# A two-layer masked attention kernel: TensorE's order fixed with projections between attention stages, units of eight heads, transposed value product

## The chip, the cores and the metric

One NeuronCore of one Trainium2 chip runs the kernel. The metric is the device time of one execution in microseconds; the kernel before takes 4095.5 us (median of 4 runs, 4094.55 to 4097.6).

TensorE does the matrix products and the transposes, VectorE, ScalarE and GpSimd the rest. The traces list each engine's instructions in an order of its own and put a wait down to the engine that ended it: the transposes of the probabilities, for one, waited 124.5 us in the kernel before, 122.3 of them for ScalarE. In both kernels TensorE writes its results to buffers in PSUM; the copy out of one is called an eviction below, and the program uses the buffer again only after it.

## The reference, cut to what matters

128 batches of 128 tokens with 512 features pass two layers, all in f32:

```python
# layer 0: 4 heads of 64
q, k, v = split_heads(x @ Wq), split_heads(x @ Wk), split_heads(x @ Wv)
sim  = where(adj, q k^T / 8, -max);  out = softmax(sim) v
x = layernorm(x + out @ Wo + bo)
# layer 1: 8 heads of 64, with a norm in front and the diagonal always allowed
h = layernorm(x) * gamma + beta
q, k, v = split(h @ w_qkv.T)
scores = where(adj | eye, q k^T / 8, -1e9);  out = softmax(scores) v
x = layernorm(x + out @ w_out.T + b_out)
```

## The kernel before

Four batches (512 tokens) form a group, and there are 32 groups. The tokens of a group are transposed to xT, projected to qk and v, and then every batch goes through stages: scores and softmax, transposes of the probabilities, value product, transposes of its result, output product with the norm. Layer 0 of one group runs in turns with layer 1 of the group before it. A scheduler, which works with its own guess of times, puts every engine's instructions in order.

```python
def scores(l, g, b):
    ...
    for h in range(H):
        nc.tensor.matmul(ps[:, h % 2, h // 2, :], qk[r, h // 2, t], qk[r, H // 2 + h // 2, t], ...)
    nc.gpsimd.memset(sm, (NEG0, NEG1)[l])
    for s in range(2):
        nc.vector.copy_predicated(sm[:, s], mask..., ps[:, s, :H // 2, :])
    nc.vector.tensor_reduce(nmax, sm, AX.X, ALU.max, negate=True)
    ... # one Exp per head on ScalarE, with its sum
def attend(l, g, b):
    for h in range(H):
        nc.tensor.matmul(pm[:, h * D:(h + 1) * D], pT[:, h, :], v[:, b, h * D:(h + 1) * D], ...)
    nc.vector.tensor_mul(a..., pm..., rec...)
def attended_t(l, g, b):
    ... # TensorE transposes of a, ScalarE copies them to aT
def residual(l, g, b):
    nc.gpsimd.tensor_tensor(xb, xin, (bias0, bias1)[l], op=ALU.add)
    ... # output product: aT, WO
    nc.vector.tensor_add(y, pm, xb)
    norm_stats(y, 0, mv)
    r = rstd_of(mv, 1)                      # two small GpSimd instructions
    nc.vector.tensor_scalar(y, y, mv[:, 0, 0:1], r, op0=ALU.subtract, op1=ALU.mult)
STAGES = (scores, probs_t, attend, attended_t, residual)
```

## Time and profile before

| engine | busy us | share | instructions |
|---|---|---|---|
| TensorE, matmuls | 3890.9 | 95% | 16193 |
| VectorE | 1654.0 | 40% | 3366 |
| ScalarE | 1139.0 | 28% | 4013 |
| GpSimd | 755.3 | 18% | 1095 |

TensorE's busy time here says how long something was in it, not how fast it went: 3891 us busy, where its instructions at their undisturbed distances make 3523 (the sum is told below). So two further things are read below: what the idle time before an instruction was waiting for, and the clock that TensorE was granted (mean 0.967 before). In the traces of both kernels the clock is either full or half (1.0 or 0.5 in all 132 records before and 258 after), so the time at half clock is about 2 x (1 - mean) x span: 2 x 0.033 x 4095 = 270 us before.

Here are two groups of the view of groups. The columns are: line, engine, operation, tiles, shape and count; busy us and mean ns of one; idle time of the engine before them, and what ended it.

```profile
L252 PE MATMUL o<-wo,aT 128*128 128x512 f32 x1536 | 768.3, 630 | 2.6 <-ACT aT L226 1.8 <-DVE x L255 0.8
...
L259 DVE TENSOR_SCALAR x<-x,mv,rstd 128x512 f32<-128x512 f32 x128 | 68.8, 537 | 48.1 <-POOL rstd L239 48.1
```

The output product (o) hardly ever waits, and VectorE's normalizing instruction takes 537 ns.

### The profile page before, as it was taken

The numbers are of one execution on the slowest core, as the hardware profiler recorded it, in microseconds if no ns is written. First come the engines' busy times: TensorE is split into PE (matmuls) and PEld (weight loads), VectorE is DVE, ScalarE is ACT, GpSimd is POOL, SyncE is SP. The second block draws the span as 40 slices with busy tenths as digits, with TensorE's granted clock in tenths as the row PEclk, the third lists the DMA queues.
The fourth block names the chain that finished last, engine by engine and source line by source line (L and its number), as shares of the span: only waits on it lengthen the run. The fifth ranks groups of instructions, "written<-read, shape, count | busy, mean of one in ns | idle before, by whom it ended". The sixth has DMA issues, their size and how long they took to land.

```text
span 4094.8 us, 42881 instructions
## 1 busy us (share of the span) xinstructions
PE 3890.9 (95%) x16193; PEld 2270.6 (55%) x16193; DVE 1654.0 (40%) x3366; ACT 1139.0 (28%) x4013; POOL 755.3 (18%) x1095
## 2 busy tenths in 40 slices
PE   8999999999999999999999999999999999999998
PEld 5555555555555555555555555555555555555554
DVE  3343443434434334334344343443434434334443
ACT  2322322223323133232232222322313323223222
POOL 1121211212212112112121121221211211112120
PEclk8999999999999999999999999999999999999998
DMA  3000000000000000000000000000000000000000
GB/s 100 12 22 11 22 17 17 22 11 22 22 14 19 16 17 22 17 17 22 11 22 17 16 22 11 22 19 14 22 11 22 22 14 19 21 12 22 6 13 14
DMA packets 56894, 78.78 MB, mean 19 GB/s; under 512 B 19816, under 2 KB 21360, under 8 KB 56688
## 3 DMA queue, kind: packets, MB, share of 16 engines
q1 hardware_dynamic: 56688, 76.04, 5.4%
q8 instruction: 128, 2.10, 0.2%
q14 instruction: 78, 0.64, 0.1%
HBM read 42.47 MB, written 33.55 MB: 19 GB/s over the span
## 4 chain that ended last, share of the span: by engine, by line
PE 72%; DVE 13%; POOL 7%; ACT 4%; issue 3%; DMA 1%; POOLq 0%; ACTq 0%
PE qk L134 33%; PE v L148 16%; PE o L252 8%; PE av L211 4%; PE xt L118 3%; PE sc L170 3%; DVE sm L175 3%; ACT sm L182 3%; PE pt L196 3%; POOL rstd L239 3%; POOL xb L249 2%; DVE nmax L178 2%; POOL sm L173 2%; DVE h L271 1%; DVE y L255 1%
## 5 line engine op out<-in xcount | busy, mean ns | idle before, releaser
L134 PE MATMUL qk<-xT,w 128*128 128x512 f32 x3072 | 1364.2, 601 | 0.0
L134 PEld LDWEIGHTS qk<-xT,w 128*128 128x128 f32 x3072 | 582.1, 193 | 674.9 <-issue 665.1
L249 POOL TENSOR_TENSOR xb<-x,bias 128x512 f32<-128x512 f32 x256 | 324.4, 1267 | 2776.4 <-DVE x L255 1577.2
L252 PE MATMUL o<-wo,aT 128*128 128x512 f32 x1536 | 768.3, 630 | 2.6 <-ACT aT L226 1.8
L182 ACT ACTIVATE sm<-sm,nmax 128x128 f32<-128x128 f32 x1536 | 595.0, 390 | 462.5 <-DVE nmax L178 461.4
L148 PE MATMUL v<-w,xT 128*128 128x256 f32 (+1 forms) x2048 | 670.9, 486 | 0.0
L148 PEld LDWEIGHTS v<-w,xT 128*128 128x128 f32 x2048 | 389.1, 190 | 285.0 <-issue 260.2
L141 DVE COPY qk<-qk 128x512 f32<-128x512 f32 x96 | 66.4, 692 | 959.5 <-PE qk L134 959.5
L196 PE MATMUL pt<-ident,sm 128*128 128x128 f32 x1536 | 317.9, 306 | 124.5 <-ACT sm L182 122.3
L150 DVE COPY v<-v 128x512 f32<-128x512 f32 x192 | 132.8, 692 | 747.4 <-PE v L148 747.4
L226 ACT COPY aT<-at 128x256 f32<-128x256 f32 (+1 forms) x256 | 121.8, 476 | 1117.1 <-PE at L224 1116.6
L252 PEld LDWEIGHTS o<-wo,aT 128*128 128x128 f32 x1536 | 288.3, 203 | 253.4 <-issue 230.8
L211 PE MATMUL av<-v,pT 128*128 128x64 f32 x3072 | 378.2, 274 | 0.2 <-DVE pT L202 0.2
L211 PEld LDWEIGHTS av<-v,pT 128*128 128x128 f32 x3072 | 369.6, 195 | 1.2 <-DVE pT L202 0.9
L196 PEld LDWEIGHTS pt<-ident,sm 128*128 128x128 f32 x1536 | 202.0, 154 | 272.9 <-ACT sm L182 188.5
L170 PE MATMUL sc<-qk 64*128 64x128 f32 x3072 | 319.4, 299 | 1.7 <-DVE sm L175 1.7
L175 DVE COPY_PREDICATED sm<-m,sc 128x256 f32<-128x256 uint8 (+1 forms) x512 | 283.0, 574 | 39.1 <-PE sc L170 35.8
L182 ACT ACTIVATION_READ_ACCUMULATOR sm<-sm,nmax 128x1 f32 x1536 | 289.8, 189 | 0.0
L170 PEld LDWEIGHTS sc<-qk 64*128 64x128 f32 x3072 | 233.7, 187 | 57.4 <-issue 27.8
L173 POOL MEMSET sm<- 128x512 f32 (+1 forms) x256 | 197.9, 773 | 301.9 <-PE pt L196 301.6
L178 DVE TENSOR_REDUCE nmax<-sm 128x4 f32<-128x512 f32 (+1 forms) x256 | 240.8, 940 | 3.3
L137 ACT ACTIVATE qk<-qk 128x512 f32<-128x512 f32 x192 | 114.6, 597 | 424.5 <-PE qk L134 424.5
(45 smaller groups left out, 2217.4 us busy)
## 6 DMA issues: line engine op xcount, KB each, us to landing
x<-in_x_dram SPq DMA_DIRECT2D x32, 1024.0 KB, 5.3
out_dram<-y SPq DMA_DIRECT2D x128, 256.0 KB, 2.0
w_qkv<-in_L_gnn_w_qkv_dram SPq DMA_DIRECT2D x12, 256.0 KB, 2.7
m<-in_adj_dram SPq DMA_DIRECT2D x32, 64.0 KB, 2.1
w_out<-in_L_gnn_w_out_dram SPq DMA_DIRECT2D x4, 256.0 KB, 2.7
w<-in_L_gnn_Wq_dram SPq DMA_DIRECT2D x1, 512.0 KB, 6.4
w<-in_L_gnn_Wk_dram SPq DMA_DIRECT2D x1, 512.0 KB, 7.3
w<-in_L_gnn_Wv_dram SPq DMA_DIRECT2D x1, 512.0 KB
```

The source lines that it names most:

```text
L134: nc.tensor.matmul(pm, W[l][:, c, f * P:(f + 1) * P], xT[:, c, :], start=(c == 0), stop=(c == KC - 1))
L148: nc.tensor.matmul(pm[:, (b - b0) * I:(b - b0 + 1) * I], xT[:, c, b * N:(b + 1) * N], W[l][:, c, 2 * I:3 * I], start=(c == 0), stop=(c == ...
L150: nc.vector.tensor_copy(v[:, b0:b0 + per, :], pm.rearrange("p (b i) -> p b i", i=I))
L170: nc.tensor.matmul(ps[:, h % 2, h // 2, :], qk[r, h // 2, t], qk[r, H // 2 + h // 2, t], start=True, stop=True)
L173: nc.gpsimd.memset(sm, (NEG0, NEG1)[l])
L175: nc.vector.copy_predicated(sm[:, s], mask[:, None, :].to_broadcast([P, H // 2, N]), ps[:, s, :H // 2, :])
L178: nc.vector.tensor_reduce(nmax, sm, AX.X, ALU.max, negate=True)
L182: nc.scalar.activation(sm[:, s, k, :], sm[:, s, k, :], AF.Exp, bias=nmax[:, s, k:k + 1], accum_out=total[:, s, k:k + 1])
L196: nc.tensor.transpose(pt[:, (h - h0) * N:(h - h0 + 1) * N], sm[:, h % 2, h // 2, :], ident)
L211: nc.tensor.matmul(pm[:, h * D:(h + 1) * D], pT[:, h, :], v[:, b, h * D:(h + 1) * D], start=True, stop=True)
L249: nc.gpsimd.tensor_tensor(xb, xin, (bias0, bias1)[l], op=ALU.add)
L252: nc.tensor.matmul(pm, aT[:, c * P:(c + 1) * P], WO[l][:, c, :], start=(c == 0), stop=(c == nk - 1))
```

## The change

Its intent is to keep TensorE fed: its order is taken from the program and no longer from the scheduler. Projection steps of other groups ("fill") are laid between the attention stages. Eight heads form a unit, which is one batch of layer 1 or two of layer 0. Each of the six slots per group handles three units at three stages. The value product takes V as weights, so that its result comes out transposed and needs no transposes; the reciprocal of the softmax then has to be applied earlier, and GpSimd does it. The core of the diff:

```diff
+    ctx.enter_context(tc.manual_schedule(engines={PE}))
...
+        nc.gpsimd.memset(sm, (NEG0, NEG1)[l])
...
+        for s in range(2):
+            nc.vector.copy_predicated(sm[:, s]..., mask..., ps[:, s]...)
+            nc.vector.tensor_reduce(nmax[:, s], sm[:, s], AX.X, ALU.max, negate=True)
+            for i in range(4):
+                nc.scalar.activation(sm[:, s, i, :], sm[:, s, i, :], AF.Exp, bias=nmax[:, s, i:i + 1],
+                                     accum_out=total[:, s, i:i + 1])
+            nc.vector.reciprocal(rec[:, s], total[:, s])
+            nc.gpsimd.tensor_tensor(sm[:, s], sm[:, s], rec[:, s, :, None].to_broadcast([P, 4, N]),
+                                    op=ALU.mult)
...
+        for i, (b, hp) in enumerate(pairs(u)):
+            for s in range(2):
+                h = 2 * hp + s
+                nc.tensor.matmul(pa[s * D:(s + 1) * D, i, :], V[l, g][:, b, h * D:(h + 1) * D],
+                                 pT[:, s, i, :], start=True, stop=True)
+        aT = two.tile([P, 4, N], F32, tag="aT", name=f"aT{name}")
+        nc.scalar.copy(aT, pa)
...
-            nc.tensor.matmul(pm[:, h * D:(h + 1) * D], pT[:, h, :], v[:, b, h * D:(h + 1) * D],
-                             start=True, stop=True)
-        nc.vector.tensor_mul(a.rearrange("p (h d) -> p h d", d=D), ...
-    def attended_t(l, g, b):
...
+    def slot(u, fill):
+        stages = ((scores, u, 0.4), (attend, recent[1], 0.2), (residual, recent[1], 0.2),
+                  (probs_t, recent[0], 0.2))
+        ... # after each stage, that share of the slot's fill steps
```

In the two slots of layer 0 the fill is the layer-1 projection (some 26 steps each). In the four slots of layer 1 it is the layer-0 projection of the next group and the transposes of h (7 steps each). The pre-norm of layer 1 is now taken batch by batch, right behind the norm of layer 0.

## The prediction

> **What bounds the kernel now.** I read the page first. TensorE is busy for nearly the whole span, every other engine for less than half of it.
>
> ```profile
> span 4094.8 us, 42881 instructions
> PE 3890.9 (95%) x16193; PEld 2270.6 (55%) x16193; DVE 1654.0 (40%) x3366; ACT 1139.0 (28%) x4013; POOL 755.3 (18%) x1095
> PE qk L134 33%; PE v L148 16%; PE o L252 8%; PE av L211 4%; PE xt L118 3%; PE sc L170 3%; DVE sm L175 3%; ACT sm L182 3%; PE pt L196 3%; POOL rstd L239 3%; POOL xb L249 2%; DVE nmax L178 2%; POOL sm L173 2%; DVE h L271 1%; DVE y L255 1%
> ```
>
> The third line is the chain that ended last. It lies on TensorE for the projections, but it leaves TensorE in the softmax (sm, nmax) and in the norms (rstd, xb, y, h). So TensorE is the bound except in the attention, where others pass work round it. How much it loses there I read from the start-to-start distances in TensorE's timeline, in a stretch of layer 1 (columns: start, length, engine, line, operation, count, idle time before it):
>
> ```profile
> 2082.11 13.04 PE L134 MATMUL qk<-xT,w 128*128 128x512 f32 x30
> 2094.99 7.07 PE L148 MATMUL v<-w,xT 128*128 128x256 f32 x32
> 2101.89 3.60 PE L252 MATMUL o<-wo,aT 128*128 128x512 f32 x8
> 2105.33 0.60 PE L224 MATMUL at<-ident,a 128*128 128x128 f32 x4
> 2105.76 1.90 PE L211 MATMUL av<-v,pT 128*128 128x64 f32 x16
> 2107.50 1.05 PE L196 MATMUL pt<-ident,sm 128*128 128x128 f32 x8
> 2108.47 0.71 PE L170 MATMUL sc<-qk 64*128 64x128 f32 x8
> ...
> 2126.81 1.00 PE L211 MATMUL av<-v,pT 128*128 128x64 f32 x8
> 2127.74 0.72 PE L170 MATMUL sc<-qk 64*128 64x128 f32 x8
> 2131.07 0.33 PE L196 MATMUL pt<-ident,sm 128*128 128x128 f32 x1 [2.61 <-ACT sm L182]
> ```
>
> qk: 30 in 2094.99 - 2082.11 = 12.88 us, 0.429 us each (512 columns); v of layer 0: 0.216 (256 columns); a transpose: 0.109 (128 columns); av: 16 in 1.74 us, about 0.11 each although only 64 columns pass[...]. Every f32 matmul is two such instructions, a transpose one. The last line is a bubble: nothing is left to issue while the softmax runs.
>
> Per group of four batches (32 groups) these distances give: qk 96 x 0.429 = 41.2; v 32 x 0.429 + 32 x 0.216 = 20.6; o 48 x 0.429 = 20.6; transposes of x and h 32 x 0.109 = 3.5, of the probabilities 48 x 0.109 = 5.2, of the attended rows 24 x 0.109 = 2.6; av 96 x 0.112 = 10.8; scores 96 x 0.056 (they run as pairs) = 5.4. Sum 110 us, against 4095 / 32 = 128 us. So about 18 us a group (some 560 us in all) are bubbles and changes of mode.
>
> [...] eight score instructions of 128 columns take 0.65 us (2115.36 to 2116.01), changes of mode included, less than eight transposes (0.97). For columns no run here shows it yet. [...] The av of eight before scores takes 0.93 us (2126.81 to 2127.74), before a transpose 0.84 (2119.98 to 2120.82): about 0.1 us per entry, and I take the same for the exit. [...] 95% busy, yet 110 of 128 us.
>
> **Removed.** The 768 transposes of the attended rows with their copies (2.6 us of TensorE per group); the multiplication by the reciprocal on VectorE (87.0 + 52.5 us in all, off the path). The value product becomes 64 x 128 with V as the weights: 64 columns to load, 128 to pass, in two column halves. If the halves run together like the scores, 0.056 each: 96 x 0.056 = 5.4 instead of 10.8. **Added.** On GpSimd a multiplication of 128x512 twice per unit of eight heads: 12 x 1.27 us (as xb, L249) = 15 us per group; it lay at 755 / 32 = 24 and comes to some 41 with the separate statistics of the pre-norm, off the path as long as it only feeds the next slot. **Moved.** Evictions are shared between ScalarE and VectorE. TensorE's order is now fixed: each of six slots per group has scores (8 matmuls) | fill | value product of two units ago | fill | its output product | fill | transposes of the previous unit | fill, so the softmax has a slot to finish. This removes the bubbles of the last line above.
>
> TensorE's work per group after: 110 - 2.6 - 5.4 = 102, plus 0.2 us for each of 12 visits to a tiled mode = 2.4; I take 1.2 us for scores and 1.1 for the value product of a unit: 41.2 + 20.6 + 20.6 + 8.7 + 6 x 2.3 = 104.9 us. If nothing waited: 32 x 104.9 = 3357 us.
>
> **The new wait.** In the order in which the changed kernel is built, ScalarE has in every slot the eight exponentials of the *current* unit in front of the copy aT of the unit whose output product TensorE wants in the *same* slot. From the end of the scores: copy_predicated twice 0.62, max twice 0.59 (the last counted to its end, 0.68, with 0.1 of signal), so the first exponential after the first max at about 2.1; eight exponentials with their accumulator reads at 0.386 each (rows L182: starts 2004.40, 2004.80, 2005.18) = 3.1; aT 0.58: output product at about 5.9 us. TensorE has until there, in a layer-1 slot, three fill steps (2 matmul instructions each, 0.86): 2.57, value product 1.1, one step 0.86 = 4.5. In the layer-0 slots it has ten steps or more, no wait. So:
> - Layer-1 slot 0: waits 5.9 - 4.5 = 1.4 us.
> - Slots 1 and 2: the norms of layer 0's output stand in VectorE's order ahead of copy_predicated: y, x1 and h of two batches, with four trips to GpSimd for rstd (0.22 + 0.57 each, behind xb 1.26 and memset 0.92). Counted row by row from the end of the previous output product, copy_predicated starts at 6.5 to 7, the last exponential ends at 12, the product can start at 12.6; TensorE's own work up to there is 9.2. Wait 3.4. In slot 2 the first transposes of h wait for the last h (8.0), and ScalarE has their eviction (0.77) ahead of the exponentials and one of qk ahead of aT: start at 14.1 against 8.8, wait 5.3.
> - Slot 3: no norms of layer 0, but an eviction of 0.68 ahead of aT, and less fill: 10.9 against 8.4, wait 2.5.
> Sum 12.6 us per group, 31 x 12.6 = 390 us. Ends: 9 us until the first qk (as before), weight transposes 7 plus some 10 of waiting for their two buffers, the last group's units without fill some 20, last norm 10: 56. Total 3357 + 390 + 56 = 3803; I take 3815 for the signals I have not counted.
>
> **Rivals.** (a) Everything is hidden: 3357 + 56, about 3415. For it: idle engines at 40 and 28%. Against: [...] four L1 slots with only 4.5 us of fill. (b) The column halves don't run together: each of 16 instructions takes about 0.11, or up to 0.16 if loads aren't hidden. In layer-1 slots it lies inside the wait; in the 64 layer-0 slots it adds 0.9 to 1.6 us: 3815 + 60 to 100. (c) GpSimd's multiplications slow VectorE and stretch the norm chain: two or three microseconds more in slots 1 and 2, 3815 + 130 to 190. (d) The fixed order is worse than the scheduler's, every slot waiting for a PSUM buffer (scores have one instead of two): 4095 or more. Against: the scores' buffer is read within 1.5 us and wanted again 12 us later, and the bubble sum before is 560 us, more than my waits.
>
> **Range and chances.** The chain in layer-1 slots is certain in kind, its length good to some 40%: 390 +/- 150. (b) and (c) push up, overlap I overlooked pushes down. 3640 to 3960. Faster by over 2% means below 4014: 0.92; same 0.06; slower 0.02.
>
> **What would show it.** TensorE's groups: no at; av near 0.06 us start to start (0.11: rival b); projections still 0.43 apart. Idle before TensorE's output product released by aT, some 8 to 12 us a group, in layer-1 slots alone; none in layer-0 slots; idle before the transposes of h released by h. ScalarE's aT copy directly behind the accumulator read of the eighth exponential. Period about 117 us per group instead of 128. I am wrong if waits for aT total under 150 us (a) or if the bubbles sit at scores or at fill matmuls (d).

## The result, and the profile after

The changed kernel takes 4199.16 us (median of 4 runs, 4196.74 to 4199.89) and the kernel before 4095.52 beside it. The ratio is 1.0251, with a 95% interval of 1.0237 to 1.0266: it is slower by 2.5%, where 3815 and "faster" had been predicted. A ratio is the mean time of one kernel's fast runs over that of the other's of the same rounds, so not quite the ratio of the medians quoted. The result is correct.

The page's engine line and chain by engine:

```profile
span 4197.0 us, 41535 instructions
...
PE 3705.4 (88%) x15425; PEld 1974.2 (47%) x15425; DVE 1700.0 (41%) x3242; ACT 1123.6 (27%) x3945; POOL 1208.2 (29%) x1608
...
PE 64%; DVE 13%; ACT 11%; POOL 9%; issue 3%; DMA 0%; ACTq 0%; POOLq 0%; DVEq 0%
```

TensorE has less work than before, as intended, but it is idle for 12% of a longer span, and the chain that ended last runs through ScalarE and VectorE for a quarter of the time. The view of groups tells where it waits:

```profile
L313 PE MATMUL o<-wo,aT 128*128 128x512 f32 x1536 | 835.0, 694 | 266.8 <-ACT aT L278 266.8
...
L275 PE MATMUL av<-pT,v 128*64 128x128 f32 x3072 | 230.9, 297 | 4.2 <-DVE pT L263 4.2
...
L298 DVE TENSOR_SCALAR x<-y,mv,rstd 128x512 f32<-128x512 f32 x128 | 100.6, 786 | 64.7 <-POOL rstd L291 64.7
...
L141 PE MATMUL xt<-ident,h 128*128 128x128 f32 x512 | 97.7, 307 | 175.5 <-DVE h L298 111.2 <-DVE pT L263 64.2
```

The value product costs little, as intended (231 us busy). The output product, which waited 2.6 us in all before, now waits 266.8 us for ScalarE's copy aT. The transposes of h wait 175.5 us for VectorE. And VectorE's normalizing instruction has become slower, 786 ns for 537.

Next, one steady group, cut into its six slots (from the end of one output product to the end of the next). The view of windows gives for each: its limits and length, the busy time of each engine with its count of instructions, the granted clock (PEclk), DMA share, GB/s. The order is layer-1 slots 2 and 3, the two layer-0 slots, layer-1 slots 0 and 1 (of the neighbouring group, so that each is whole):

```profile
2002.13:2020.24 18.11, 14.50 (x68) 7.81 (x67) 9.05 (x20) 5.38 (x20) 7.68 (x12) 0.91 0.00 0
2020.24:2036.89 16.65, 14.16 (x77) 9.21 (x76) 7.04 (x13) 5.68 (x20) 5.05 (x6) 0.90 0.05 17
2036.89:2063.12 26.23, 24.09 (x96) 13.29 (x95) 7.44 (x13) 6.89 (x22) 4.96 (x6) 0.93 0.03 11
2063.12:2091.41 28.29, 28.29 (x105) 14.01 (x104) 8.23 (x15) 6.70 (x22) 5.01 (x6) 1.00 0.03 10
2091.41:2111.00 19.59, 18.69 (x80) 9.37 (x79) 9.20 (x18) 5.41 (x20) 5.80 (x7) 1.00 0.04 15
2111.00:2131.84 20.84, 15.49 (x63) 7.52 (x62) 12.07 (x23) 4.82 (x19) 9.18 (x15) 0.84 0.16 53
```

They add up to 129.7 us. A steady group of the kernel before takes 126.3 (its whole span over 32 groups is 128), and 117 had been predicted. The long layer-0 slot (28.29 us) is full and at full clock. Layer-1 slot 1 (the last line) is the worst: 5.3 us idle and a clock of 0.84. Its TensorE timeline:

```profile
2118.40 1.09 PE L275 MATMUL av<-pT,v 128*64 128x128 f32 x16
2119.43 1.12 PE L171 MATMUL qk<-xT,w 128*128 128x512 f32 x2
2125.91 6.10 PE L313 MATMUL o<-wo,aT 128*128 128x512 f32 x8 [5.35 <-ACT aT L278]
2131.84 0.59 PE L171 MATMUL qk<-xT,w 128*128 128x512 f32 x1
```

The sixteen value-product instructions start within 1.02 us (sixteen of the kernel before took 1.74), so the two column halves do run together. Then TensorE waits 5.35 us. And the eight instructions of the output product, which ran 0.43 us apart before, now take 5.93 us from the first start to the next instruction's. By their start times they are 1.02, 0.85, 0.85, 0.85, 0.85, 0.65, 0.43 and 0.43 us apart: the first five go at half speed and the sixth in part (the granted clock is 0.59 from 2125.91 to 2131.84). ScalarE's and VectorE's lines behind that wait:

```profile
2112.39 1.48 DVE L298 TENSOR_SCALAR x<-y,mv,rstd 128x512 f32<-128x512 f32 x1 [0.51 <-POOL rstd L291]
...
2116.27 1.14 DVE L298 TENSOR_SCALAR h<-x,mvh,rstd 128x512 f32<-128x512 f32 x1 [0.42 <-POOL rstd L291]
...
2119.89 0.70 DVE L239 COPY_PREDICATED sm<-m,sc 128x512 f32<-128x512 uint8 x1
...
2122.20 0.40 ACT L245 ACTIVATE sm<-sm,nmax 128x128 f32<-128x128 f32 x1 [4.82 <-DVE nmax L243]
...
2124.91 0.39 ACT L245 ACTIVATE sm<-sm,nmax 128x128 f32<-128x128 f32 x1
2125.20 0.19 ACT L245 ACTIVATION_READ_ACCUMULATOR sm<-sm,nmax 128x1 f32 x1
2125.29 0.56 ACT L278 COPY aT<-av 128x512 f32<-128x512 f32 x1
```

The value product was done before 2120, but its copy aT stands in ScalarE's queue behind the eight exponentials of another unit. Those wait for VectorE, which comes to their copy_predicated only at 2119.89, behind the norms. And one normalizing instruction in there took 1.48 us: it started at 2112.39, just after GpSimd had begun a 1.27 us addition (xb). Another took 1.14 us, behind the start of a memset:

```profile
2112.32 1.27 POOL L310 TENSOR_TENSOR xb<-x,bias 128x512 f32<-128x512 f32 x1
...
2116.19 0.95 POOL L223 MEMSET sm<- 128x1024 f32 x1
```

**A sum over the whole trace.** For every TensorE instruction I took the distance to the start of the next one, and from it the undisturbed distance of its kind (0.429 us for 512 columns, 0.216 for 256, 0.109 for a transpose, 0.056 for scores and for the new value product, 0.112 for the old one). Of the rest, what falls into stretches at half clock is counted as clock, up to the undisturbed distance once more; what remains is waits and changes of mode:

| kernel | undisturbed | clock | waits and modes | sum | at half clock |
|---|---|---|---|---|---|
| before | 3523 | 123 | 436 | 4082 | 275 |
| changed | 3267 | 225 | 692 | 4184 | 577 |

So 256 us of work did go. The waits grew by as much, and the clock lost 102 us more.

### The profile page after: what moved, and what is told of

Its sections match the earlier page's. It is cut to its first block, busy times and chain, and to the rows that moved or that the text cites. A ratio compares the mean times of both kernels' runs of the same rounds, so it can differ in the third digit from the quotient of the medians.

```text
span 4197.0 us, 41535 instructions
## 1 busy us (share of the span) xinstructions
PE 3705.4 (88%) x15425; PEld 1974.2 (47%) x15425; DVE 1700.0 (41%) x3242; ACT 1123.6 (27%) x3945; POOL 1208.2 (29%) x1608
## 4 chain that ended last, share of the span: by engine, by line
PE 64%; DVE 13%; ACT 11%; POOL 9%; issue 3%; DMA 0%; ACTq 0%; POOLq 0%; DVEq 0%
PE qk L171 23%; PE o L313 18%; PE v L186 12%; ACT sm L245 9%; PE sc L234 4%; POOL rstd L291 4%; POOL xb L310 3%; PE pt L259 2%; DVE sm L239 2%; PE xt L141 2%; DVE st L283 2%; DVE nmax L243 2%; DVE x L298 2%; PE av L275 2%; DVE h L298 2%
## 5 line engine op out<-in xcount | busy, mean ns | idle before, releaser
L171 PE MATMUL qk<-xT,w 128*128 128x512 f32 x3072 | 1466.1, 615 | 0.0
L313 PE MATMUL o<-wo,aT 128*128 128x512 f32 x1536 | 835.0, 694 | 266.8 <-ACT aT L278 266.8
L248 POOL TENSOR_TENSOR sm<-sm,rec 128x512 f32<-128x512 f32 x384 | 396.5, 1039 | 1282.5 <-DVE rec L247 1282.0
L316 DVE TENSOR_TENSOR y<-o,xb 128x512 f32<-128x512 f32 x256 | 176.9, 691 | 911.4 <-PE o L313 908.9
L239 DVE COPY_PREDICATED sm<-m,sc 128x512 f32<-128x512 uint8 x384 | 260.2, 714 | 142.2 <-PE sc L234 138.6
L261 ACT COPY pT<-pt 128x512 f32<-128x512 f32 x192 | 112.3, 585 | 748.2 <-PE pt L259 748.2
L275 PEld LDWEIGHTS av<-pT,v 128*64 128x64 f32 x3072 | 183.9, 149 | 149.7 <-issue 144.5
L141 PE MATMUL xt<-ident,h 128*128 128x128 f32 x512 | 97.7, 307 | 175.5 <-DVE h L298 111.2
L175 ACT COPY qk<-qk 128x512 f32<-128x512 f32 x192 | 111.8, 582 | 525.2 <-PE qk L171 525.2
L243 DVE TENSOR_REDUCE nmax<-sm 128x4 f32<-128x512 f32 x384 | 245.5, 674 | 1.0
L275 PE MATMUL av<-pT,v 128*64 128x128 f32 x3072 | 230.9, 297 | 4.2 <-DVE pT L263 4.2
L223 POOL MEMSET sm<- 128x1024 f32 x192 | 182.7, 952 | 172.1 <-PE pt L259 170.9
```

The lines of the kernel that those rows point to most:

```text
L141: nc.tensor.transpose(pt[:, b * N:(b + 1) * N], src[:, b, c * P:(c + 1) * P], ident)
L171: nc.tensor.matmul(pm, W[l][:, c, f * P:(f + 1) * P], XT[l, g][:, c, :], start=(c == 0), stop=(c == KC - 1))
L239: nc.vector.copy_predicated(sm[:, s].rearrange("p (b h) n -> p b h n", h=H2), mask[:, :, None, :].to_broadcast([P, len(bs), H2, N]), ps[:, ...
L243: nc.vector.tensor_reduce(nmax[:, s], sm[:, s], AX.X, ALU.max, negate=True)
L248: nc.gpsimd.tensor_tensor(sm[:, s], sm[:, s], rec[:, s, :, None].to_broadcast([P, 4, N]), op=ALU.mult)
L275: nc.tensor.matmul(pa[s * D:(s + 1) * D, i, :], V[l, g][:, b, h * D:(h + 1) * D], pT[:, s, i, :], start=True, stop=True)
```

## The experiments

**Theory A.** What loses is where a few instructions stand in the queues of ScalarE and VectorE: aT behind the exponentials, h and pT behind the norms. Every long wait then lowers the clock, which costs again. **Rivals.** B: the low clock lies inside the waits and costs nothing. C: VectorE's norm chain is the real bound. D: the fixed order of TensorE loses by itself.

| run | what | us | ratio to before | mean clock |
|---|---|---|---|---|
| changed | | 4199.2 | 1.0251 | 0.932 |
| e1_warm | idle matmuls in the waits | 4099.2 | 1.0008 | 0.985 |
| e2_aT_first | aT ahead of the exponentials | 3939.5 | 0.9620 | 0.946 |
| e3_xt_late | transposes of h in slot 3 | 4086.7 | 0.9977 | 0.943 |
| e4_no_xb | no addition on GpSimd | 4091.7 | 0.9990 | 0.943 |
| e5_scheduled | no fixed order | 3870.9 | 0.9450 | 0.956 |
| e6_before_avT | before, with the transposed value product alone | 4188.5 | 1.0226 | 0.932 |
| e7_both | e2 and e3 together | 3753.7 | 0.9164 | 0.982 |
| e8_both_pT | e7, pT copied by ScalarE alone | 3640.9 | 0.8889 | 0.983 |
| e9_qk | e8, one more copy to ScalarE | 3649.4 | 0.8909 | 0.984 |
| e10_both_scheduled | e8 without fixed orders | 3868.6 | 0.9446 | 0.956 |
| e11_avT_dve | e6, multiplication on VectorE | 4287.5 | 1.0468 | 0.910 |

All are correct, four runs each.

**A step in these times, which I overlooked.** In the traces of the kernel before and of the changed one the stretches at half clock (66 and 129 of them) begin on a fixed grid of 3.413 us, to within 1 ns, and most last one interval (61 and 92) or, in the changed kernel, two (34). The period of a steady group is a whole number of these intervals in most kernels: 37.00 before, 38.00 changed, 37.00 in e3 and e4, 35.00 in e5 and e10, 38.00 in e6, 39.00 in e11; two groups of e2 take 71. It is not whole in e1 and e7 to e9, which lose only 35 to 48 us to the clock. One interval per group is 109 us in 32 groups. So before and changed lie one step apart, and the gains of e3 and e4 are one step each: that the time fell is shown, but its size is not the size of what was moved. Why the period locks to the grid no run here tests.

### e1_warm: keep TensorE busy while it waits

```diff
+    def warm(tile, n):
+        for _ in range(n):
+            nc.tensor.matmul(tile, wo0[:, 0, :P], wo0[:, 0, :], start=True, stop=True)
...
+            if g > 0 and j == 0 and k == 1:
+                warm(pm, 5 if l == 0 else 2)      # before the output product
...
+                if l == 1 and c == 3 and 0 < g < NG - 1:
+                    warm(ps_ao.tile([P, E], F32, tag="ao", name=f"warm{g}"), 2)
+                if l == 1 and c == 0 and 0 < g < NG - 1:
+                    warm(pt, 3)                   # before the transposes of h
```

> The changed kernel, with idle matmuls (f32, 512 columns, results overwritten) laid where TensorE only waits in a steady group: 5 before the output product in layer-1 slot 1 (it waited 5.5 us), 2 before that of slot 3 (1.9), 3 before the first transposes of h in slot 2 (3.4), 2 before the last transposes of h (2.3). Theory A (the waits themselves cost some 690 us in all, and on top of them each long wait lets the TensorE clock fall to half for 3.4 to 7 us, which costs some 225 us): the waits stay, the half-clock time falls from 577 us to under 250, and the output product after the wait in slot 1 takes 3.5 us instead of 5.9; the time falls by 100 to 180 us, to 4020 to 4100. Theory B (half clock lies inside the waits and costs nothing of its own): time unchanged within 20 us of 4199.

Measured: 4099.2 us, 100 us less, though TensorE has 734 instructions more and each result is overwritten. The mean clock rose to 0.985, so about 2 x 0.015 x 4095 = 123 us at half clock remain of 577. By the sum used above the clock's cost fell from 225 to 48 us, while waits and idle matmuls together are some 75 us longer than the waits were. The clock costs time of its own, and B falls. The effect is at the low end of what was expected. At the output products of slots 1 and 3 the clock now stayed full, but a wait grew at a place that I had not filled: the output product of slot 2, which got no idle matmuls, waited 2.2 us where it had waited 0.7, and ran at half clock (5.2 us for its eight).

### e2_aT_first: aT ahead of the exponentials

```diff
-    ctx.enter_context(tc.manual_schedule(engines={PE}))
+    ctx.enter_context(tc.manual_schedule(engines={PE, ACT}))
...                                               # scores() is cut in two; in slot():
+            if stage is attend and u is not None:
+                softmax(u)
```

> The changed kernel, with the softmax given out after the value product and ScalarE's order fixed like TensorE's, so that the copy aT stands ahead of the eight exponentials of the slot; nothing else moves. Theory A (ScalarE's order makes the output product wait): the 267 us of waits of the output product for aT fall below 50, the half-clock time behind them goes too; 3.5 to 4.5 us less in slot 1 and in slot 3 each and 1 in slot 0, in all 250 to 400 us: 3800 to 3950. The waits for h in slot 2 stay. Theory C (VectorE's norm chain is the real bound, ScalarE only shows it): TensorE stops at the transposes of the probabilities or at the scores instead, and less than 80 us are gained.

Measured: 3939.5 us, 260 us less than the changed kernel.

```profile
L322 PE MATMUL o<-wo,aT 128*128 128x512 f32 x1536 | 695.9, 596 | 5.9 <-ACT aT L287 5.9
...
L142 PE MATMUL xt<-ident,h 128*128 128x128 f32 x512 | 102.1, 301 | 346.4 <-DVE h L307 282.1 <-DVE pT L272 64.2
```

The wait of the output product for aT is gone, 5.9 us for 266.8. That ScalarE's order made it is thereby shown: TensorE's order is the same in both traces (the scheduler also moved a few instructions of VectorE and GpSimd). But the transposes of h now wait 346.4 us, twice as long: I had expected theirs to stay as they were. TensorE reaches them sooner, and h is not ready sooner. That is C's cause, at a place which C had not named, and the gain is over three times what C allowed.

### e3_xt_late: the transposes of h later

```diff
-            fill = fill[:half] + (interleaved(fill[half:], transposed_steps(1, g)) if fill
-                                  else [None] * 0 + transposed_steps(1, g))
+            fill = fill + transposed_steps(1, g)
```

> The changed kernel, with the transposes of h moved behind the layer-0 projections, into slot 3, where h has long been ready. Theory A: the 121 us of waits of the transposes for h vanish, ScalarE's exponentials in slot 2 no longer stand behind the eviction of the first transpose (2 us earlier), the half clock after it goes (1.3 to 2 us): 3 to 5 us per group, 4040 to 4110. If the wait is only handed on to aT in the same slot (it could start no earlier than about 12.4 us after the previous output product, now 14.6): the lower gain of 2 us, 4130.

Measured: 4086.7 us, 112 us less, within what theory A gave.

```profile
L313 PE MATMUL o<-wo,aT 128*128 128x512 f32 x1536 | 880.0, 726 | 368.1 <-ACT aT L278 368.1
...
L141 PE MATMUL xt<-ident,h 128*128 128x128 f32 x512 | 76.1, 280 | 15.7 <-DVE h L298 11.7 <-ACT xT L148 0.5
```

The waits of the transposes of h fell from 175.5 to 15.7 us in the view of groups; those of the output product for aT rose from 266.8 to 368.1. So about a hundred microseconds of the wait were handed on, and the gain is what the earlier exponentials, the pT waits and the clock (0.943 for 0.932) leave.

### e4_no_xb: no addition on GpSimd

```diff
-            nc.gpsimd.tensor_tensor(xb, xin, (bias0, bias1)[l], op=ALU.add)
-            nc.vector.tensor_add(y, pm, xb)
+            nc.vector.tensor_add(y, pm, xin)
```

> The changed kernel without the bias addition on GpSimd: y is the product plus x directly. (The output biases are zero in these inputs, so the result stays right; as a kernel it would be wrong for others.) Theory A2 (VectorE's normalizing instructions on SBUF are held while GpSimd works: they take 1086 ns in the mean when GpSimd is busy at their start, 624 otherwise): their mean falls from 780 to about 600 ns, the norm chain in slots 1 and 2 shortens by 1 to 2 us each, time 4060 to 4150. Theory B2 (the norm chain is made of its trips to GpSimd alone, the additions are beside the path): unchanged within 30 us.

Measured: 4091.7 us, 107 us less; the additions were on the path, and B2 falls.

```profile
L298 DVE TENSOR_SCALAR h<-x,mvh,rstd 128x512 f32<-128x512 f32 x128 | 89.0, 695 | 53.6 <-POOL rstd L291 53.6
L298 DVE TENSOR_SCALAR x<-y,mv,rstd 128x512 f32<-128x512 f32 x128 | 71.5, 558 | 60.3 <-POOL rstd L291 60.2
```

The x rows, which met the addition, fell from 786 to 558 ns; the h rows (698 before, 695 now), which meet the memset (in the timeline of slot 1), did not; the y rows fell from 847 to 709. The mean of all three is 654 ns, not the 600 expected. Both halves of the norm chain were helped here, the held instructions and the trips for rstd behind xb in GpSimd's queue; this run doesn't part them, and as the gain is one step of the grid, 107 us is not their size.

### e5_scheduled: no fixed order

```diff
-    ctx.enter_context(tc.manual_schedule(engines={PE}))
```

> The changed kernel without the fixed order of TensorE: the same instructions, buffers and units, put in order by the scheduler on every engine, as in the kernel before. Rival D (the fixed order of TensorE is itself what loses): clearly under 4095, some 3900. Theory A (what loses is where the copy aT, the norms and h stand in the queues of ScalarE and VectorE, and the scheduler works with its own guess of times): TensorE may fill some waits with other projections, but waits of the same kind remain, 4000 to 4250.

Measured: 3870.9 us. This is D's number, and theory A's range was missed. The waits are of the same kind, only smaller (the output product waits 132.8 us for aT, with ScalarE's queue still holding four or eight exponentials before most copies). In the trace the scheduler has put three projection steps in front of the output product in slot 0 where the fixed order has one, and has laid transposes of h and layer-0 projections into other waits. So in the changed kernel the fixed order does lose 330 us. Whether it loses by itself is what e10 asks.

### e6_before_avT and e11_avT_dve: one part of the change alone

```diff
+            nc.gpsimd.tensor_tensor(sm[:, s], sm[:, s], rec[:, s, :, None].to_broadcast([P, H // 2, N]),
+                                    op=ALU.mult)          # e11: nc.vector in place of nc.gpsimd
...
-            nc.tensor.matmul(pm[:, h * D:(h + 1) * D], pT[:, h, :], v[:, b, h * D:(h + 1) * D],
+            nc.tensor.matmul(pm[r, h // 2 * N:(h // 2 + 1) * N], v[:, b, h * D:(h + 1) * D], pT[:, h, :],
...
-STAGES = (scores, probs_t, attend, attended_t, residual)
+STAGES = (scores, probs_t, attend, residual)
```

> The kernel before with one part of the change alone: the value product transposed in two column halves, the probabilities multiplied by the reciprocal on GpSimd, no transposes of the attended rows; batches as units, order by the scheduler. By TensorE's sum it saves 2.6 + 5.4 us per group less 0.2 us for each of 8 entries into the column mode: 6.4 us x 32 = 205 us, 3890. Rival: GpSimd's multiplication (1.04 us per half) lengthens the softmax before the transposes of the probabilities, where the kernel before already has its bubbles: 8 batches x up to 2 us = 16 us per group would eat all of it, 4095 to 4400; half of it hidden, 4050.

> The kernel before with the transposed value product alone (4189 us with the multiplication on GpSimd), the multiplication moved to VectorE. If its loss comes from GpSimd's 1.04 us per half (and its queue) between the exponentials and the transposes of the probabilities (309 us of waits for it), VectorE's 0.6 us halves that: 4000 to 4080, under 4095. If it comes from having the multiplication in that path at all, or from the lost cover of the transposes of the attended rows: 4120 to 4200.

Measured: 4188.5 and 4287.5 us, both slower than the kernel before. First the row of e6, then that of e11:

```profile
L198 PE MATMUL pt<-ident,sm 128*128 128x128 f32 x1536 | 320.8, 335 | 310.8 <-POOL sm L187 309.0 <-DVE gb L106 0.3
```

```profile
L198 PE MATMUL pt<-ident,sm 128*128 128x128 f32 x1536 | 316.2, 341 | 333.2 <-DVE sm L187 331.6 <-DVE gb L106 0.3 <-DVE mv L222 0.2
```

In the kernel before, this wait was 124.5 us, for ScalarE. In the old order nothing covers a longer softmax, so the multiplication eats the 256 us of TensorE's work that the transposed product saves. So e6 lies where its rival had put it. e11 lies outside both of its ranges. My reason, that GpSimd is slow at it, falls: on VectorE it takes less (615 ns in the mean of both shapes, where GpSimd took 830), but the wait is as long and the clock lower (0.910). What is left is the multiplication standing in that path at all, or the lost cover of the transposes of the attended rows; no run parts these. The 99 us between e6 and e11 are one step of the grid, with 773 us at half clock for 570; what pushed e11 over it I have not settled. The part paid only in kernels with units of eight heads (e2, e5, e7 to e10).

### e7_both and e8_both_pT: the repairs together

```diff
+            fill = fill[:21] + (interleaved(fill[21:], transposed_steps(1, g)) if fill
+                                else transposed_steps(1, g))       # e7, on top of e2
...
-            if s:
+            if True:                                               # e8: pT
                 nc.scalar.copy(pT[:, s], pt.rearrange("p (i n) -> p i n", n=N))
```

> The changed kernel with both repairs: aT ahead of the exponentials, and the transposes of h among the last layer-0 projection steps, in slot 3. With aT first the transposes of h waited 346 us and the clock stayed at half for 424 us; theory A says that both waits were the loss and that nothing else stands behind them: TensorE's 3267 us, some 230 us of mode changes, start, end and small waits, 70 us of waits of the last transposes of h for VectorE's copy pT: 3570 to 3650. Theory C (VectorE's norm chain takes over again, at the transposes of the probabilities or the scores): 3700 to 3850.

> The last kernel with both halves of the transposed probabilities evicted by ScalarE, so that no transpose waits for a buffer that VectorE frees only behind a norm's trip to GpSimd. Theory A: the 64 to 70 us of waits for the copy pT vanish and with them the half clock behind: 60 to 110 us under the kernel with both repairs. Rival: ScalarE, with 6 more copies of 0.48 us per group, delays aT or the next exponentials: no gain, or up to 50 us lost.

Measured: 3753.7 and 3640.9 us. e7 missed theory A's range by 104 us and lies in that of C: behind the two waits stood more of them:

```profile
PE av L284 <- DVE pT L272: 67.9, 62, 2.4
PE xt L142 <- DVE pT L272: 58.2, 30, 1.9
PE v L187 <- DVE qk L178: 55.2, 30, 1.9
```

That is (waiter, releaser, us in total, times, longest) 67.9 us of the value product and 58.2 us of the transposes of h for VectorE's copy pT, 55.2 us of v for VectorE's copy of qk. All three are copies standing behind norms in VectorE's queue, so C was right that VectorE takes over, at other places than it named. e8 took the pT copies out of that queue, which gave 113 us, a little more than expected. (The scheduler also let copy_predicated pass a norm there; the two are not parted.) By the sum used above it has 3267 us undisturbed, 36 clock and 323 waits and modes. It beats both kernels: 0.8889 of before (interval 0.8875 to 0.8902).

### e9_qk: one more copy

```diff
-                    if f % 2:
+                    if f % 2 or (l == 0 and f == 2):
                         nc.scalar.copy(QK[l, g][:, f, :], pm)
```

> The last repaired kernel (3641 us), with the third qk tile of layer 0 evicted by ScalarE too: in its trace the first v matmul of layer 0 waited 2.6 us per group (78 us in all) for VectorE's copy of that tile, which stands behind the norms. Theory A (each wait is an order in a queue and can be moved): 78 us less, 3560. Rival: ScalarE takes the copy up only behind the eight exponentials of that slot, and the wait is the same from another engine: 3620 to 3660.

Measured: 3649.4 us, no gain; the rival was right. The 78 us of waits for that copy went, and 61.3 us of waits of transposes for ScalarE's copy pT and 46.9 us of the probabilities' transposes for ScalarE's copy xT came. Moving copies to ScalarE is at its end here.

### e10_both_scheduled: the repaired kernel without fixed orders

```diff
-    ctx.enter_context(tc.manual_schedule(engines={PE, ACT}))
```

> The repaired kernel of 3641 us without any fixed order: TensorE and ScalarE are ordered by the scheduler again, all else as there. Rival D (a fixed order of TensorE loses by itself): at or under 3641. Theory A (a fixed order is good once the other queues fit it; the scheduler puts aT among the exponentials again): 3680 to 3850, with waits of the output product for aT of 50 us or more.

Measured: 3868.6 us, 228 us slower than e8.

```profile
L321 PE MATMUL o<-wo,aT 128*128 128x512 f32 x1536 | 806.0, 674 | 260.7 <-ACT aT L286 260.7
```

The scheduler lays aT behind three to five of the eight exponentials again in the layer-1 slots, and the old wait is back at 260.7 us; the time is 19 us above theory A's range. So D falls as a general statement: with ScalarE's queue in the order that fits, the fixed order is the fastest version seen; with TensorE's alone fixed, it is the slowest of the three versions with these units (4199, 3871, 3641). These three differ in more than the orders, and as e10 lets go both engines at once, it doesn't tell their shares.

## Why the prediction was wrong

**TensorE's work: right.** Undisturbed it went from 3523 to 3267 us, 102 us per group as predicted. Its count of instructions holds: an f32 product is two (o x1536 for 768 products), a transpose one (pt x1536). The column halves run together: 16 instructions in 1.02 us, so rival (b) is out; its "up to 0.16" each was the author's estimate. This is the case of which the prediction could show no run. Entries and exits cost about 0.1 us each, as taken: a qk instruction ahead of the value product lasts 0.523 us in the median in place of 0.429, and from the last score instruction to the start of a projection it is 0.202, where the second of a pair of scores otherwise takes 0.105.

**The new wait: right in kind, and in place but for layer 0.** The prediction named the order on ScalarE; that ScalarE would take up aT only behind the exponentials was its author's assumption, and the trace shows it (product done before 2120, aT started at 2125.29). The waits of the steady group, read from the start times, are:

| slot | waits predicted | measured | clock, not predicted |
|---|---|---|---|
| layer 1, slot 0 | 1.4 | 1.1 | 0 |
| layer 1, slot 1 | 3.4 | 5.5 | 2.5 |
| layer 1, slot 2 | 5.3 | 3.3 for h, 0.7 for aT | 1.7 |
| layer 1, slot 3 | 2.5 | 2.1 for aT, 0.7 for a buffer | 1.8 |
| layer 0, first slot | 0 | 2.3 for pT | 1.6 |
| layer 0, second slot | 0 | 0 | 0 |
| sum | 12.6 | 15.7 | 7.6 |

With the 104.9 us of work these make 128.2 of the measured 129.7 us; the rest is small.

**The step that failed: "3357 + 390 + 56".** It took every TensorE instruction at its undisturbed distance, as if a wait cost only itself. The trace shows more: after the waits of 2.1 us and more 512 columns take 0.853 us in place of 0.429, and 577 us pass at half clock. Half clock followed all 30 waits of 2.1 us (slot 3), all 30 of 2.3 us (first layer-0 slot), of 3.3 us (slot 2) and of 5.5 us (slot 1), but of 32 of 1.1 us before an output product (slot 0) only two. Half clock costs 7.6 us in the group above (225 us in the sum over the whole trace), the largest missing term; the waits were 3.1 us a group larger than predicted, some 96 us. The kernel before had the same thing, unseen by me, in its "18 us of bubbles and changes of mode": 123 us of its 560 are clock, most of it behind waits of the probabilities' transposes of 2.8 and 1.3 us (30 of 30 each), not behind 29 of 1.1 us. e1 shows that the clock costs by itself: waits filled with useless work, 100 us gained. Together 3357, waits of 487 (31 x 15.7) and 225 for the clock make 4069 of the 4197 us; the ends took some 71 where 56 were predicted, and small waits the rest.

**"Counted row by row": mis-sized in slot 1 by 2 us.** The norm chain was counted from the kernel before, where a normalizing instruction takes 537 to 591 ns in the mean and GpSimd is 18% busy. Now they take 786, 847 and 698 ns in the mean (x, y, h). The 128 that started while GpSimd was at work took 1086 ns in the mean, and their length follows what remains of GpSimd's instruction (correlation 0.998). The trace shows this as a hold until GpSimd's instruction ends, for the additions and the fills: 34 that started under an addition xb took 1483 ns in the mean and 62 under a memset 1144, and both ended 0.28 us in the median after it; those that met no GpSimd work took 546 ns in the median. The statistics do not change: in the kernel before, 189 that started while GpSimd worked took 682 ns in the mean, the others 679. In slot 1 one x was held by xb (1.48 us) and one h by a memset (1.14), and copy_predicated began 8.9 us after the output product's end, not 6.5 to 7. This was rival (c), which I gave GpSimd's new multiplications; in slot 1 it was the old addition and the memset, met at a worse time. e4 shows that the addition is on the path.

**"In the layer-0 slots it has ten steps or more, no wait": wrong at one place.** That is true of aT. But the last transposes of h need a PSUM buffer that VectorE's copy pT frees, and pT stands behind a norm that waits for GpSimd's rstd: 2.3 us in each group, and the clock after it. I had checked the scores' buffers and not these. e7 to e8 shows that moving pT pays: 113 us, though more of the waits that went were the value product's (67.9 us) than the transposes' (58.2).

**Rival (d)** came nearest in its number (4095 or more), but not by its mechanism: the scores waited 1.5 us in all for their single PSUM buffer. By e2, e5 and e10, what makes the fixed order lose is that the other engines' queues are ordered by a guess that doesn't fit it; a run with ScalarE's order alone fixed was not made. "Overlap I overlooked" worked the other way.

**Of the change as a whole:** the transposed product takes out 256 us of TensorE's work, which e6 alone could not keep; the slots could keep it, if aT, h and pT were put where TensorE finds them ready (e8). Left open: how much of e4's gain is the hold and how much GpSimd's queue; why e11 is worse than e6; why the group's period locks to the clock's grid; and what the fixed order of TensorE and that of ScalarE each contribute in e8.

## What to carry to other kernels

When one engine's order is fixed by hand, look up in the built order of every other engine what stands in front of the one copy that the fixed engine will want next; here the copy aT of 0.56 us stood behind eight exponentials, and the output product waited 5.35 us for it. Count for each long wait of TensorE also the work behind it at half clock, here half of the wait again (7.6 us on 15.7; after all waits of 2.1 us and more in the steady groups of the changed kernel). Look at the clock's grid before you give a small gain a size: here the periods of eight of the thirteen kernels were a whole number of intervals of 3.413 us. And fill moved from a full slot to a starved one, or an instruction moved within a queue, was worth more here (558 us from 4199 to 3641) than the arithmetic saved (256 us).
